# Two-layer mixture-of-experts kernel, first layer's conditioner: load order, sums by parts, slot computation inside the units, three shared blocks behind the pairs

## The chip, the cores and the metric

The kernel runs on one core of one Trainium2 chip. The metric is the device time of one execution in microseconds; the median of three runs stands for the kernel. The profile is of one further execution, whose own time is given beside its span, the time from its first to its last instruction.

## The reference

x holds 32 batches of 128 tokens of width 128. There are two layers, each a conditioner and an FFN, and each adds its result to x. The change touches layer 0's conditioner and its border to layer 0's FFN:

```python
def _L0_cond_ref(context_c, time_cond, ...):
    head, wrist, proprio = context_c[:, :42], context_c[:, 42:84], context_c[:, 84:]
    full_agg = context_c.mean(axis=1)
    hp_agg = concatenate([head, proprio], axis=1).mean(axis=1)
    wp_agg = concatenate([wrist, proprio], axis=1).mean(axis=1)
    gate_logits = concatenate([full_agg, hp_agg, wp_agg], -1) @ gate_w + gate_b
    scale, shift = split(silu(time_cond) @ time_w + time_b, 2, -1)
    gate_scores = softmax(gate_logits * (1.0 + scale) + shift)
    topk_w, topk_i = top_k(gate_scores, 2)          # two of four experts per batch
    topk_w = topk_w / (topk_w.sum(-1) + 1e-08)
    for e in range(4):
        y = gelu(context_c @ ew1[e] + eb1[e]) @ ew2[e] + eb2[e]
        out = out + w_be[:, e] * mask[e] * y        # w_be: topk_w, zero where not chosen
    shared = gelu(context_c @ sw1 + sb1) @ sw2 + sb2
    return out + shared

def _L0_ffn_ref(x, w_router, w_gating, w_gate, w_up, w_down):   # eight experts, all used
    cw = softmax(x @ w_router) * softmax(x @ w_gating / 0.1)
    cw = cw / (sum(cw, -1) + 1e-09)
    return sum over e of cw[:, :, e] * ((silu(x @ w_gate[e]) * (x @ w_up[e])) @ w_down[e])
```

Layer 1 (a second conditioner with routed experts, and a low-rank FFN) is not touched.

## The kernel before

All activations lie transposed, 128 features on the partitions. x is eight blocks of 512 columns, each four batches; `xT[b]` is a block of x, `c0T[b]` the block of the conditioner's output that the FFN reads. All matmuls are in 32-bit floats, so that one matmul of the source is two passes in the trace.

Layer 0's conditioner is a list of units, run by `pipelined`: the up-projection of the next unit is issued before the down-projection of the present one, so that TensorE has matmuls to do while ScalarE works out the GELU. A shared unit (`"s", b`) takes one block through the shared expert: four matmuls (`hidden`, L203, tiles us), each followed by a GELU on ScalarE (L204), then four matmuls summed into one PSUM tile (`project`, L209, tile ys), which VectorE writes to `c0T` (L227). A pair unit (`"p", q`) takes two batches of 128 tokens through one routed expert. Which batches and which expert is only known at run time: 34 pairs of slots are filled from the gates, and the batches' columns are gathered by VectorE (`gather`, L367) and the expert's weights fetched by SyncE's DMA (`fetch`, L357, 578 KB each, three ahead) at addresses held in registers. Results are multiplied by the gate and added to `c0T` (L395).

Slots come from a chain of small steps. `sums` (L197) adds up each batch of x over all tokens, over head with proprio, and over wrist with proprio, as the tokens are sorted head, proprio, wrist. `cond_gates` multiplies these by the gate weights (the gate group on TensorE: gate_ps, mod_ps, t_ps), takes the softmax with an Exp on ScalarE (L257) and chooses two of four (mask, L175). `schedule` counts the choices with two small matmuls (order_ps, L281 and L282), works out each slot's batch, expert and gate on VectorE (up to L321) and spreads them with one matmul (slots_ps, L324) before they are turned to integers (L325 to L328). `spread_times` (tl_ps, L341) prepares a term for layer 1.

The units are shared blocks 0 to 6, the 34 pairs, and shared block 7. The steps of the slot chain are called between units by `after_l0`, after the unit's down-projection: the gates after block 2, the schedule and the first three fetches after block 3, the times after block 4, the first gathers after block 5. Block 7 comes behind the pairs, so its `c0T` begins as zero and its result is added (L225).

The FFN follows: `logits_ahead` (lg_ps, L421) projects blocks 0 to 3 on the gate weights, `ffn_logits` transposes that back (lg_b, L436), `ffn_gates` takes the softmaxes and their product, `gates_to_dram` transposes the result (fg_ps, L450) and stores it, and `fetch_rows` reads it back by rows. Before the change these are called in front of, within and after the first two units of the FFN. 64 FFN units (block, expert) follow, each with eight matmuls up and four down.

Each engine works through its own instructions in order; the order on each engine is set by a scheduler when the kernel is built, near the order of the source. PSUM tiles rotate: six of tag mm (all up-projections and all small matmuls) and two of tag y.

Of the kernel before, what the change touches and what calls it, by code (L numbers as in the profile page):

```python
# [35 lines left out]
ALU = mybir.AluOpType  # L36
AX = mybir.AxisListType
# [54 lines left out]
def adaln_ffn(  # L92
# [19 lines left out]
    def const(shape, name, dtype=F32):  # L112
        return cpool.tile(shape, dtype, tag=name, name=name)
# [14 lines left out]
    c0T = [c0all[:, b * TB : (b + 1) * TB] for b in range(NB)]  # L128
    ident = const([P, P], "ident")

    nc.scalar.dma_start(out=par, in_=packed)
    nc.sync.dma_start(out=xT[0], in_=x[0])
    nc.scalar.dma_start(out=sw1_t, in_=sw1)
    nc.sync.dma_start(out=sw2_t, in_=sw2.rearrange("(c p) d -> p c d", p=P))
    for blk in range(1, NB):
        nc.sync.dma_start(out=xT[blk], in_=x[blk])
    nc.sync.dma_start(out=rows, in_=row.partition_broadcast(P))
    nc.sync.dma_start(out=ident, in_=eye)
# [49 lines left out]
    cT = par[:, AT["cond"]]  # L188
    sT = const([P, B], "sT")
    nc.scalar.activation(sT, cT, AF.Silu)  # L190
    full, hp, wp = (const([P, B], n) for n in ("full", "hp", "wp"))

    def sums(blk):
        xb = batches(xT[blk])
        at = slice(blk * BB, (blk + 1) * BB)
        for to, (lo, hi) in ((full, (0, S)), (hp, NO_WRIST), (wp, NO_HEAD)):
            V.tensor_reduce(to[:, at], xb[:, :, lo:hi], AX.X, ALU.add)  # L197


    def hidden(ps, h, rhs, w, bias):  # L200

        for c in range(NC):
            nc.tensor.matmul(ps[c], lhsT=w[:, c * P : (c + 1) * P], rhs=rhs, start=True, stop=True)  # L203
            nc.scalar.activation(h[:, c, :], ps[c], AF.Gelu_apprx_tanh, bias=bias[:, c : c + 1])  # L204

    def project(w, h, n, name):
        y = y_tile(name)
        for c in range(NC):
            nc.tensor.matmul(y[:, :n], lhsT=w[:, c, :], rhs=h[:, c, :n], start=(c == 0), stop=(c == NC - 1))  # L209
        return y  # L210

    LAST = NB - 1

    def shared_up(blk):
        h = work.tile([P, NC, TB], F32, tag="h", name=f"hs0_{blk}", bufs=3)
        ps = [mm_tile(f"us_{blk}_{c}") for c in range(NC)]
        hidden(ps, h, xT[blk], sw1_t, col("sb1", 0, NC))
        for b in range(3 * blk, min(3 * blk + 3, NB)):
            sums(b)
        return h  # L220

    def shared_down(blk, h):
        y = project(sw2_t, h, TB, f"ys_{blk}")
        if blk == LAST:
            V.scalar_tensor_tensor(c0T[blk], y, col("sb2"), c0T[blk], ALU.add, ALU.add)  # L225
        else:
            V.tensor_scalar(c0T[blk], y, col("sb2"), None, ALU.add)  # L227
# [4 lines left out]
    tsb = const([B, E1], "tsb")  # L232

    def cond_gates():
        V.tensor_scalar(full, full, 1.0 / S, None, ALU.mult)
        V.tensor_scalar(hp, hp, 1.0 / NSEEN, None, ALU.mult)
        V.tensor_scalar(wp, wp, 1.0 / NSEEN, None, ALU.mult)
        gps = mm_tile("gate_ps")
        for i, agg in enumerate((full, hp, wp)):
            nc.tensor.matmul(  # L240
                gps[:B, :E0], lhsT=agg, rhs=col("gate_w", i * E0, E0), start=(i == 0), stop=(i == 2)
            )
        mps = mm_tile("mod_ps")
        nc.tensor.matmul(mps[:B, : 2 * E0], lhsT=sT, rhs=col("time_w", 0, 2 * E0), start=True, stop=True)
        tps = mm_tile("t_ps")
        nc.tensor.matmul(tps[:B, :E1], lhsT=cT, rhs=col("r1t", 0, E1), start=True, stop=True)
        V.tensor_copy(tsb, tps[:B, :E1])
        mod = const([B, 2 * E0], "mod")
        stat = const([B, 4], "stat")
        V.tensor_tensor(gl2, gps[:B, :E0], rows[:B, ATROW["gate_b"]], ALU.add)  # L250
        V.tensor_tensor(mod, mps[:B, : 2 * E0], rows[:B, ATROW["time_b"]], ALU.add)
        V.tensor_scalar(mod[:, :E0], mod[:, :E0], 1.0, None, ALU.add)
        V.tensor_tensor(gl2, gl2, mod[:, :E0], ALU.mult)
        V.tensor_tensor(gl2, gl2, mod[:, E0:], ALU.add)
        V.tensor_reduce(stat[:, 0:1], gl2, AX.X, ALU.max)
        V.tensor_scalar(gl2, gl2, stat[:, 0:1], None, ALU.subtract)
        nc.scalar.activation(gl2, gl2, AF.Exp)  # L257
        V.tensor_reduce(stat[:, 1:2], gl2, AX.X, ALU.add)
        V.reciprocal(stat[:, 2:3], stat[:, 1:2])
        V.tensor_scalar(gl2, gl2, stat[:, 2:3], None, ALU.mult)  # L260
        chosen = top2(gl, B, 1, E0, "c")
        V.tensor_tensor(gl, gl, chosen, ALU.mult)
        V.tensor_reduce(stat[:, 3:4], gl2, AX.X, ALU.add)
        V.tensor_scalar(stat[:, 3:4], stat[:, 3:4], 1e-08, None, ALU.add)
        V.reciprocal(stat[:, 2:3], stat[:, 3:4])
        V.tensor_scalar(gl2, gl2, stat[:, 2:3], None, ALU.mult)

        return chosen.rearrange("p o e -> p (o e)")

# [1 line left out]
    batch_at = const([1, NSLOT], "batch_at", I32)  # L273
    expert_at = const([1, NPAIR + 2], "expert_at", I32)

    def schedule(chosen):


        ps = mm_tile("order_ps")
        earlier = par[:B, AT["earlier"]]  # L280
        nc.tensor.matmul(ps[:B, :E0], lhsT=earlier, rhs=chosen, start=True, stop=True)  # L281
# [19 lines left out]
        shape = [B, E0, NSLOT]  # L301
        at = const(shape, "at")
        part = const(shape, "part")
        sums = const([B, 2 * NSLOT + NPAIR], "sums")
        V.tensor_tensor(
            at, pos.unsqueeze(2).to_broadcast(shape),
            par[:B, AT["slot"]].unsqueeze(1).to_broadcast(shape), ALU.is_equal,
# [11 lines left out]
        V.tensor_scalar(pairs, first[:, 1, :], float(P), None, ALU.mult)  # L319
        for e in range(2, E0):  # L320
            V.scalar_tensor_tensor(pairs, first[:, e, :], float(e * P), pairs, ALU.mult, ALU.add)  # L321
        ps = mm_tile("slots_ps")
        n = sums.shape[-1]
        nc.tensor.matmul(ps[:, :n], lhsT=ones, rhs=sums, start=True, stop=True)  # L324
        V.tensor_copy(batch_at, ps[:1, NSLOT : 2 * NSLOT])  # L325
        V.tensor_copy(expert_at[:, :NPAIR], ps[:1, 2 * NSLOT : n])
        V.tensor_copy(expert_at[:, NPAIR:], ps[:1, n - 2 : n])
        V.tensor_copy(gate_of, ps[:, :NSLOT])  # L328

    tl = const([P, B, E1], "tl")  # L330

# [41 lines left out]
    def pair_up(q):  # L373
        if q + NW - 1 < NPAIR:
            fetch(q + NW - 1)
        if q + AHEAD < NPAIR:
            gather(q + AHEAD)
        w, x = weights[q], slots.pop(q)
        h = work.tile([P, NC, 2 * S], F32, tag="h", name=f"h0_{q}", bufs=3)
        ps = [mm_tile(f"u_{q}_{c}")[:, : 2 * S] for c in range(NC)]  # L380
        hidden(ps, h, x.rearrange("p s t -> p (s t)"), w[:, ATP["w1"]], w[:, ATP["eb1"]])
        return h

    def pair_down(q, h):
# [7 lines left out]
        for i, at in enumerate(batch.pop(q)):  # L392
            acc = c0all[:, bass.ds(at, S)]
            s = 2 * q + i
            V.scalar_tensor_tensor(acc, t[:, i, :], gate_of[:, s : s + 1], acc, ALU.mult, ALU.add)  # L395

    def after_l0(kind, i):
        if (kind, i) == ("s", 2):
            held["chosen"] = cond_gates()
        if (kind, i) == ("s", 3):  # L400
            schedule(held["chosen"])
            for q in range(NW - 1):
                fetch(q)
        if (kind, i) == ("s", 4):
            spread_times()
        if (kind, i) == ("s", 5):
            for q in range(AHEAD):
                gather(q)

    held, in_dram = {}, {}  # L410
    L0 = {"s": (shared_up, shared_down), "p": (pair_up, pair_down)}
    units = [("s", b) for b in range(LAST)] + [("p", q) for q in range(NPAIR)] + [("s", LAST)]
    nc.gpsimd.memset(c0T[LAST], 0.0)
    pipelined(units, lambda k, i: L0[k][0](i), lambda k, i, h: L0[k][1](i, h), after_l0)

    lg = const([P, NT, 2 * EF], "lg")

# [69 lines left out]
        )  # L487
        held["f", sb] = cwT


    def fetch_rows(blk):

        sb, j = divmod(blk, SB)
        t = work.tile([P, 2, TB], F32, tag="gT", name=f"fgT{blk}")
        for k in range(4):
            nc.sync.dma_start(
                out=t[32 * k : 32 * k + 1, :, :], in_=in_dram["f", sb][k : k + 1, :, j * TB : (j + 1) * TB]
            )
        return t

    def spread(row, name):

# [6 lines left out]
        nc.scalar.activation(s, ps_gate, AF.Silu)  # L509
        V.tensor_tensor(h, s, ps_up, ALU.mult)  # L510

    fgates = {}
    l1 = const([P, NT, E1], "l1")

    def ffn_up(blk, e):
        h = work.tile([P, NC, TB], F32, tag="h", name=f"hf_{blk}_{e}", bufs=3)
        for c in range(NC):
            if (blk, e, c) == (0, 0, 1):
                ffn_logits(0)
            cs = slice(c * P, (c + 1) * P)  # L520
            g, u = mm_tile(f"g_{blk}_{e}_{c}"), mm_tile(f"u_{blk}_{e}_{c}")
            nc.tensor.matmul(g, lhsT=wg_t[:, e, cs], rhs=c0T[blk], start=True, stop=True)  # L522
            nc.tensor.matmul(u, lhsT=wu_t[:, e, cs], rhs=c0T[blk], start=True, stop=True)  # L523
            glu(g, u, h[:, c, :], f"sf_{blk}_{e}_{c}")
        if (blk, e) == (0, 0):
            ffn_gates(0)
        if (blk, e) == (0, 1):
            gates_to_dram("f", 0)
            fgates[0] = fetch_rows(0)
        return h  # L530

    def ffn_down(blk, e, h):
# [72 lines left out]
        V.tensor_scalar(flat[:, : 4 * 32], ps[:, : 4 * 32], 0.125, None, ALU.mult)  # L605
        V.tensor_scalar(flat[:, 4 * 32 :], ps[:, 4 * 32 : 12 * 32], 0.25, None, ALU.mult)

    logits_ahead("lg", par[:, AT["wr"]], c0T, 0)
    pipelined([(b, e) for b in range(NB) for e in range(EF)], ffn_up, ffn_down, after_ffn)


# [200 lines left out]
```

## Time and profile before

| | |
|---|---|
| median of three runs | 1021.22 us (1020.12 to 1021.42) |
| profiled execution, its own time | 1021.55 us |
| its span | 1019.6 us |
| TensorE busy | 1004.8 us, 99% |
| VectorE busy | 460.4 us, 45% |
| ScalarE busy | 332.6 us, 33% |
| GpSimd busy | 145.7 us, 14% |
| mean granted TensorE clock | 0.997 |
| read from HBM | 31.76 MB |

In the profile's rows PE is TensorE, PEld its weight loads, DVE VectorE, ACT ScalarE, POOL GpSimd and SP SyncE; a q behind the name is the engine's sequencer, which issues DMAs. L209 is line 209 of the kernel. A row of the timeline is a start, a length, the engine, the line, the operation, its output and inputs with their shapes, how many instructions it stands for, and in brackets how long the engine had been idle and what ended that. The stages of the span are: the conditioner of layer 0 up to about 186 us (shared blocks to 58 us, pairs to 183 us), the FFN up to 853 us, layer 1 from there.

### The profile page before, as it was taken

To read this page: it belongs to the slowest core of one execution; us is meant where nothing else is said; L and a number is where in the kernel's file an instruction comes from. 1 tells how busy PE (TensorE), PEld (TensorE's weight loads), DVE (VectorE), ACT (ScalarE), POOL (GpSimd) and SP (SyncE) were. 2 spreads that over 40 slices of the span, in tenths; PEclk is the share of its full clock that TensorE was granted. 3 is DMA by queue.
4 is the path that set the end of the run, shared out by engine and by line. 5 is a ranking of instruction groups with operands and counts; after the bars stand their busy time and mean duration, and the time that the engine had idled before them with its cause. 6 is when DMAs were issued, how large, how long until landed. Compare 5 with 4: busy or idle time off the path is not lost.

```text
span 1019.6 us, 10200 instructions
## 1 busy us (share of the span) xinstructions
PE 1004.8 (99%) x3662; PEld 478.4 (47%) x3662; DVE 460.4 (45%) x811; ACT 332.6 (33%) x575; POOL 145.7 (14%) x142
## 2 busy tenths in 40 slices
PE   7999999999999999999999999999999999999997
PEld 3368888444445444444444444444444443333341
DVE  5434443445443444333445534344433344638692
ACT  4444544423221222222223222222222222335764
POOL 0000000031111111111111101111111002008770
PEclk9999999999999999999999999999999999999999
DMA  9335555100000000000000000000000000000002
GB/s 315 106 103 179 165 176 167 34 2 1 3 2 0 1 0 1 1 1 1 0 1 1 1 3 1 0 1 0 1 0 1 0 1 3 2 6 1 2 1 82
DMA packets 18705, 34.76 MB, mean 34 GB/s; under 512 B 1680, under 2 KB 9872, under 8 KB 18640
## 3 DMA queue, kind: packets, MB, share of 16 engines
q1 hardware_dynamic: 17792, 32.61, 9.9%
q10 hardware_dynamic: 864, 1.52, 0.4%
q8 instruction: 28, 0.46, 0.2%
q14 instruction: 21, 0.17, 0.1%
HBM read 31.76 MB, written 2.36 MB: 33 GB/s over the span
## 4 chain that ended last, share of the span: by engine, by line
PE 98%; DVE 1%; DMA 0%; DVEq 0%; issue 0%; ACTq 0%
PE yf L209 22%; PE g L522 22%; PE u L523 22%; PE u L203 6%; PE y L209 6%; PE ur L625 5%; PE us L203 3%; PE g L625 3%; PE u L625 3%; PE ys L209 2%; PE p_ps L619 2%; PE ul L676 1%; PE q_ps L619 1%; DMA sw_t<-in_sw 0%; PE fold_ps L603 0%; PE o_ps L691 0%
## 5 line engine op out<-in xcount | busy, mean ns | idle before, releaser
L509 ACT ACTIVATE sf<-g 128x512 f32<-128x512 f32 x256 | 152.6, 597 | 495.5 <-PE g L522 494.3
L510 DVE TENSOR_TENSOR hf<-sf,u 128x512 f32<-128x512 f32 x256 | 175.7, 687 | 207.2 <-PE u L523 206.2
L522 PE MATMUL g<-c0all,wg_t 128*128 128x512 f32 x512 | 261.6, 592 | 0.0
L523 PE MATMUL u<-c0all,wu_t 128*128 128x512 f32 x512 | 261.4, 592 | 0.0
L209 PE MATMUL yf<-hf,wd_t 128*128 128x512 f32 x512 | 230.5, 593 | 0.0
L504 POOL PARTITION_BROADCAST fg<-fgT x64 | 77.8, 1227 | 721.1 <-DVE tf L536 516.6
L209 PEld LDWEIGHTS yf<-hf,wd_t 128*128 128x128 f32 x512 | 97.1, 190 | 123.0 <-issue 123.0
L523 PEld LDWEIGHTS u<-c0all,wu_t 128*128 128x128 f32 x512 | 97.3, 190 | 122.4 <-issue 120.3
L522 PEld LDWEIGHTS g<-c0all,wg_t 128*128 128x128 f32 x512 | 96.7, 190 | 120.5 <-issue 118.3
L536 DVE TENSOR_TENSOR tf<-yf,fg 128x512 f32<-128x512 f32 x64 | 44.2, 691 | 167.5 <-PE yf L209 162.0
L504 POOL PARTITION_BROADCAST rg<-grows x64 | 66.7, 1168 | 123.3 <-DVE hr L659 73.5
L204 ACT ACTIVATE h<-u,w 128x256 f32<-128x256 f32 x136 | 58.5, 473 | 62.2 <-PE u L203 62.2
L659 DVE TENSOR_TENSOR hr<-ar,rg 128x512 f32<-128x512 f32 x64 | 59.9, 981 | 15.9 <-ACT ar L658 15.4
L203 PE MATMUL u<-x,w 128*128 128x256 f32 x272 | 64.3, 379 | 0.0
L209 PE MATMUL y<-h,w 128*128 128x256 f32 x272 | 64.3, 379 | 0.0
L625 PE MATMUL ur<-xall,rw_t 128*32 128x512 f32 x512 | 58.4, 592 | 0.0
L203 PEld LDWEIGHTS u<-x,w 128*128 128x128 f32 x272 | 51.7, 190 | 7.9 <-issue 1.0
L209 PEld LDWEIGHTS y<-h,w 128*128 128x128 f32 x272 | 51.7, 190 | 7.4 <-issue 0.5
L658 ACT ACTIVATE ar<-ur 128x512 f32<-128x512 f32 x64 | 37.9, 598 | 27.6 <-PE ur L625 27.3
L537 DVE TENSOR_TENSOR xall<-xall,tf 128x512 f32<-128x512 f32 x64 | 45.4, 709 | 2.1
L625 PE MATMUL g<-xall,sws_t 128*32 128x512 f32 x256 | 42.0, 593 | 0.0
L625 PE MATMUL u<-xall,sws_t 128*32 128x512 f32 x256 | 42.0, 592 | 0.0
(168 smaller groups left out, 449.6 us busy)
## 6 DMA issues: line engine op xcount, KB each, us to landing
w<-in_experts SPq DMA_DIRECT2D x34, 578.5 KB
xall<-in_x SPq DMA_DIRECT2D x8, 256.0 KB
wg_t<-in_w_gate SPq DMA_DIRECT2D x8, 256.0 KB
wu_t<-in_w_up SPq DMA_DIRECT2D x8, 256.0 KB
wd_t<-in_w_down SPq DMA_DIRECT2D x8, 256.0 KB
rw_t<-in_r_w SPq DMA_DIRECT2D x2, 512.0 KB
out<-fin SPq DMA_DIRECT2D x4, 256.0 KB
out<-fin ACTq DMA_DIRECT2D x4, 256.0 KB
```

The lines of the kernel that those rows point to most:

```text
L203: nc.tensor.matmul(ps[c], lhsT=w[:, c * P : (c + 1) * P], rhs=rhs, start=True, stop=True)
L204: nc.scalar.activation(h[:, c, :], ps[c], AF.Gelu_apprx_tanh, bias=bias[:, c : c + 1])
L209: nc.tensor.matmul(y[:, :n], lhsT=w[:, c, :], rhs=h[:, c, :n], start=(c == 0), stop=(c == NC - 1))
L504: nc.gpsimd.partition_broadcast(bc, row)
L509: nc.scalar.activation(s, ps_gate, AF.Silu)
L510: V.tensor_tensor(h, s, ps_up, ALU.mult)
L522: nc.tensor.matmul(g, lhsT=wg_t[:, e, cs], rhs=c0T[blk], start=True, stop=True)
L523: nc.tensor.matmul(u, lhsT=wu_t[:, e, cs], rhs=c0T[blk], start=True, stop=True)
L536: V.tensor_tensor(t, y, spread(fgates[blk][32 * k : 32 * k + 1, g, :], f"fg_{blk}_{e}"), ALU.mult)
L537: V.tensor_tensor(xT[blk], xT[blk], t, ALU.add)
L625: nc.tensor.matmul(ps[own, :], lhsT=w[:, own], rhs=x, start=True, stop=True)
L659: V.tensor_tensor(h[:, j, :], a, gate, ALU.mult)
```

## The change

It has four parts.

1. First loads: on ScalarE's queue sw1 is issued before par (the packed small inputs); on SyncE's queue x's second block is issued before sw2.
2. Sums: each block is summed over head, proprio and wrist apart, in all of blocks 0 to 3 with shared unit 0 and 4 to 7 with shared unit 1; three additions form the three sums that the gates need.
3. Steps between: a table `between` names points inside a unit, ahead of a given chunk of a given up- or down-projection, and the steps are called there. The gates are called in the middle of block 2's up-projection, the schedule ahead of block 3's up-projection, the slots' spreading (now `spread_slots`, with the fetches and the gathers) ahead of the last chunk of block 2's down-projection, the times inside block 3's down-projection.
4. Order of units: blocks 0 to 4, the pairs, then blocks 5, 6 and 7. Three blocks begin as zeros and are added to. The FFN's first gates are worked out within these three units instead of in the first FFN units.

```diff
+    nc.scalar.dma_start(out=sw1_t, in_=sw1)
+    nc.sync.dma_start(out=xT[0], in_=x[0])
     nc.scalar.dma_start(out=par, in_=packed)
-    nc.sync.dma_start(out=xT[0], in_=x[0])
-    nc.scalar.dma_start(out=sw1_t, in_=sw1)
+    nc.sync.dma_start(out=xT[1], in_=x[1])
     nc.sync.dma_start(out=sw2_t, in_=sw2.rearrange("(c p) d -> p c d", p=P))
-    for blk in range(1, NB):
+    for blk in range(2, NB):
...
-        for to, (lo, hi) in ((full, (0, S)), (hp, NO_WRIST), (wp, NO_HEAD)):
-            V.tensor_reduce(to[:, at], xb[:, :, lo:hi], AX.X, ALU.add)
+        lo = 0
+        for to, n in ((head, NHEAD), (prop, NPROP), (wrist, NHEAD)):
+            V.tensor_reduce(to[:, at], xb[:, :, lo : lo + n], AX.X, ALU.add)
+            lo += n
...
+    between = {}
+
+    def before(*point):
+        for do in between.pop(point, ()):
+            do()
...
         for c in range(NC):
+            before("up", *unit, c)
             nc.tensor.matmul(ps[c], lhsT=w[:, c * P : (c + 1) * P], rhs=rhs, start=True, stop=True)
...
         for c in range(NC):
+            before("down", *unit, c)
             nc.tensor.matmul(y[:, :n], lhsT=w[:, c, :], rhs=h[:, c, :n], start=(c == 0), stop=(c == NC - 1))
...
-        for b in range(3 * blk, min(3 * blk + 3, NB)):
-            sums(b)
+        if blk < 2:
+            for b in range(4 * blk, 4 * blk + 4):
+                sums(b)
...
     def cond_gates():
+        V.tensor_tensor(hp, head, prop, ALU.add)
+        V.tensor_tensor(wp, wrist, prop, ALU.add)
+        V.tensor_tensor(full, hp, wrist, ALU.add)
...
+    def spread_slots():
         ps = mm_tile("slots_ps")
...
         V.tensor_copy(gate_of, ps[:, :NSLOT])
+        for q in range(NW - 1):
+            fetch(q)
+        for q in range(AHEAD):
+            gather(q)
...
-    def after_l0(kind, i):
-        if (kind, i) == ("s", 2):
-            held["chosen"] = cond_gates()
-        if (kind, i) == ("s", 3):
-            schedule(held["chosen"])
-            for q in range(NW - 1):
-                fetch(q)
-        if (kind, i) == ("s", 4):
-            spread_times()
-        if (kind, i) == ("s", 5):
-            for q in range(AHEAD):
-                gather(q)
-    units = [("s", b) for b in range(LAST)] + [("p", q) for q in range(NPAIR)] + [("s", LAST)]
-    nc.gpsimd.memset(c0T[LAST], 0.0)
...
+    def first_rows():
+        gates_to_dram("f", 0)
+        fgates[0] = fetch_rows(0)
+
+    between.update({
+        ("up", "s", 2, 2): [cond_gates],
+        ("up", "s", 3, 0): [schedule],
+        ("down", "s", 2, 3): [spread_slots],
+        ("down", "s", 3, 1): [spread_times],
+
+        ("up", "s", FIRST + 1, 2): [lambda: logits_ahead("lg", par[:, AT["wr"]], c0T, 0)],
+        ("down", "s", FIRST, 0): [lambda: ffn_logits(0)],
+        ("down", "s", FIRST, 3): [lambda: ffn_gates(0)],
+        ("down", "s", FIRST + 1, 0): [first_rows],
+    })
+    units = [("s", b) for b in range(FIRST)] + [("p", q) for q in range(NPAIR)]
+    units += [("s", b) for b in range(FIRST, NB)]
+    for b in range(FIRST, NB):
+        nc.gpsimd.memset(c0T[b], 0.0)
...
-            if (blk, e, c) == (0, 0, 1):
-                ffn_logits(0)
...
-        if (blk, e) == (0, 0):
-            ffn_gates(0)
-        if (blk, e) == (0, 1):
-            gates_to_dram("f", 0)
-            fgates[0] = fetch_rows(0)
...
-    logits_ahead("lg", par[:, AT["wr"]], c0T, 0)
```

`FIRST` is `NB - 3`, block 5.

More of the change, by code (lines that the diff above doesn't have):

```diff
@@ L190, in adaln_ffn @@
     nc.scalar.activation(sT, cT, AF.Silu)
-    full, hp, wp = (const([P, B], n) for n in ("full", "hp", "wp"))
+    full, hp, wp, head, prop, wrist = (const([P, B], n) for n in ("full", "hp", "wp", "hd", "pr", "wr"))
     def sums(blk):
@@ L195, in sums, with hidden, project @@
         at = slice(blk * BB, (blk + 1) * BB)
-        for to, (lo, hi) in ((full, (0, S)), (hp, NO_WRIST), (wp, NO_HEAD)):
-            V.tensor_reduce(to[:, at], xb[:, :, lo:hi], AX.X, ALU.add)
-    def hidden(ps, h, rhs, w, bias):
+        lo = 0
[6 more added lines that the diff above has]
+            do()
+    def hidden(ps, h, rhs, w, bias, unit):
         for c in range(NC):
+            before("up", *unit, c)
             nc.tensor.matmul(ps[c], lhsT=w[:, c * P : (c + 1) * P], rhs=rhs, start=True, stop=True)
             nc.scalar.activation(h[:, c, :], ps[c], AF.Gelu_apprx_tanh, bias=bias[:, c : c + 1])
-    def project(w, h, n, name):
+    def project(w, h, n, name, unit=()):
         y = y_tile(name)
         for c in range(NC):
+            before("down", *unit, c)
             nc.tensor.matmul(y[:, :n], lhsT=w[:, c, :], rhs=h[:, c, :n], start=(c == 0), stop=(c == NC - 1))
         return y
-    LAST = NB - 1
+    FIRST = NB - 3
     def shared_up(blk):
@@ L216, in shared_up @@
         ps = [mm_tile(f"us_{blk}_{c}") for c in range(NC)]
-        hidden(ps, h, xT[blk], sw1_t, col("sb1", 0, NC))
-        for b in range(3 * blk, min(3 * blk + 3, NB)):
-            sums(b)
+        hidden(ps, h, xT[blk], sw1_t, col("sb1", 0, NC), ("s", blk))
+        if blk < 2:
+            for b in range(4 * blk, 4 * blk + 4):
+                sums(b)
         return h
     def shared_down(blk, h):
-        y = project(sw2_t, h, TB, f"ys_{blk}")
-        if blk == LAST:
+        y = project(sw2_t, h, TB, f"ys_{blk}", ("s", blk))
+        if blk >= FIRST:
             V.scalar_tensor_tensor(c0T[blk], y, col("sb2"), c0T[blk], ALU.add, ALU.add)
@@ L266, in cond_gates @@
         V.tensor_scalar(gl2, gl2, stat[:, 2:3], None, ALU.mult)
-        return chosen.rearrange("p o e -> p (o e)")
+        held["chosen"] = chosen.rearrange("p o e -> p (o e)")
     gate_of = const([P, NSLOT], "gate_of")
@@ L274, in adaln_ffn, with schedule @@
     expert_at = const([1, NPAIR + 2], "expert_at", I32)
-    def schedule(chosen):
+    slot_sums = const([B, 2 * NSLOT + NPAIR], "slot_sums")
+    def schedule():
+        chosen = held["chosen"]
         ps = mm_tile("order_ps")
@@ L303, in schedule @@
         part = const(shape, "part")
-        sums = const([B, 2 * NSLOT + NPAIR], "sums")
+        sums = slot_sums
         V.tensor_tensor(
@@ L321, in schedule @@
             V.scalar_tensor_tensor(pairs, first[:, e, :], float(e * P), pairs, ALU.mult, ALU.add)
+    def spread_slots():
         ps = mm_tile("slots_ps")
-        n = sums.shape[-1]
-        nc.tensor.matmul(ps[:, :n], lhsT=ones, rhs=sums, start=True, stop=True)
+        n = slot_sums.shape[-1]
+        nc.tensor.matmul(ps[:, :n], lhsT=ones, rhs=slot_sums, start=True, stop=True)
         V.tensor_copy(batch_at, ps[:1, NSLOT : 2 * NSLOT])
@@ L380, in pair_up @@
         ps = [mm_tile(f"u_{q}_{c}")[:, : 2 * S] for c in range(NC)]
-        hidden(ps, h, x.rearrange("p s t -> p (s t)"), w[:, ATP["w1"]], w[:, ATP["eb1"]])
+        hidden(ps, h, x.rearrange("p s t -> p (s t)"), w[:, ATP["w1"]], w[:, ATP["eb1"]], ("p", q))
         return h
@@ L395, in pair_down @@
             V.scalar_tensor_tensor(acc, t[:, i, :], gate_of[:, s : s + 1], acc, ALU.mult, ALU.add)
-    def after_l0(kind, i):
-        if (kind, i) == ("s", 2):
-            held["chosen"] = cond_gates()
-        if (kind, i) == ("s", 3):
-            schedule(held["chosen"])
-            for q in range(NW - 1):
-                fetch(q)
-        if (kind, i) == ("s", 4):
-            spread_times()
-        if (kind, i) == ("s", 5):
-            for q in range(AHEAD):
-                gather(q)
-    held, in_dram = {}, {}
-    L0 = {"s": (shared_up, shared_down), "p": (pair_up, pair_down)}
-    units = [("s", b) for b in range(LAST)] + [("p", q) for q in range(NPAIR)] + [("s", LAST)]
-    nc.gpsimd.memset(c0T[LAST], 0.0)
-    pipelined(units, lambda k, i: L0[k][0](i), lambda k, i, h: L0[k][1](i, h), after_l0)
     lg = const([P, NT, 2 * EF], "lg")
@@ L499, in fetch_rows @@
         return t
+    held, in_dram, fgates = {}, {}, {}
+    def first_rows():
[11 more added lines that the diff above has]
+    })
+    L0 = {"s": (shared_up, shared_down), "p": (pair_up, pair_down)}
+    units = [("s", b) for b in range(FIRST)] + [("p", q) for q in range(NPAIR)]
+    units += [("s", b) for b in range(FIRST, NB)]
+    for b in range(FIRST, NB):
+        nc.gpsimd.memset(c0T[b], 0.0)
+    pipelined(units, lambda k, i: L0[k][0](i), lambda k, i, h: L0[k][1](i, h))
     def spread(row, name):
@@ L510, in glu @@
         V.tensor_tensor(h, s, ps_up, ALU.mult)
-    fgates = {}
     l1 = const([P, NT, E1], "l1")
```

## The prediction

> **What bounds the kernel now.** I read the busy shares first, then TensorE's waits, then the chain of work that ended last through the first 60 us, then the windows around its one long wait.
>
> The page's head says that TensorE is the bound: it is busy for all but 14.8 us of the span.
>
> ```profile
> span 1019.6 us, 10200 instructions
> ...
> PE 1004.8 (99%) x3662; PEld 478.4 (47%) x3662; DVE 460.4 (45%) x811; ACT 332.6 (33%) x575; POOL 145.7 (14%) x142
> ```
>
> So only TensorE's idle time, and its slow time, can be won. Its waits (who waited for what: us in total, times, longest) are three:
>
> ```profile
> PE us L203 <- DMA sw_t<-in_sw: 5.7, 1, 5.7
> PE slots_ps L324 <- DVE sums L321: 2.0, 1, 2.0
> PE o_ps L691 <- DVE qT L687: 0.8, 1, 0.8
> ```
>
> The third is at the very end and not touched. The chain (start, length, what) shows the other two:
>
> ```profile
> 1.17 4.40 DMA sw_t<-in_sw
> 5.57 0.14 issue
> 5.71 8.76 PE us L203 x16
> ...
> 35.67 3.45 PE ys L209 x8
> ...
> 44.91 0.55 PE slots_ps L324 x2
> 45.46 5.33 PE us L203 x8
> 50.79 0.62 PE tl_ps L341 x2
> 51.41 3.63 PE us L203 x8
> ```
>
> The reader is to see two things. The first matmul starts at 5.71 when sw1 is in. And the same eight passes of an up-projection take 5.33 us after the slots wait and 3.63 us one unit later. The windows explain it (length, busy time by engine, granted clock, DMA share, GB/s):
>
> ```profile
> 42.94:44.91 1.97, 0.01 (x1) 0.00 (x0) 1.88 (x7) 0.00 (x0) 0.00 (x0) 1.00 0.00 0
> 43.16:46.58 3.42, 1.67 (x5) 0.97 (x6) 2.23 (x11) 0.00 (x0) 0.00 (x0) 1.00 0.00 0
> 46.58:49.99 3.41, 3.41 (x5) 1.33 (x4) 1.08 (x7) 1.58 (x3) 0.00 (x0) 0.50 0.66 232
> 50.00:53.41 3.41, 3.41 (x9) 1.35 (x8) 1.19 (x6) 1.89 (x4) 0.00 (x0) 1.00 0.97 361
> ```
>
> TensorE is idle for 1.97 us while VectorE works out the slots; for the following 3.41 us the granted clock is 0.50. So the wait costs 1.97 us and then 5.33 - 3.63 = 1.70 us more.
>
> **The change, part by part.**
>
> *First loads (-1.05 us).* On ScalarE's queue sw1 now stands ahead of par. In the chain, sw1 is issued at 1.17 behind par's 205 KB and in use 4.40 us later, at 5.57. Par alone was issued at 0.73 and used at 4.25 (row below), 3.52 us. The 256 KB behind it ended 1.32 us later, 5.2 ns per KB; so sw1, 51 KB more than par, would be in at 0.73 + 3.52 + 0.27 = 4.52 and the first matmul starts at 4.66, after the same 0.14 of issue. x's first block was in use at 4.05 with the same place on its queue, so it isn't the later one.
>
> ```profile
> 4.05 0.69 DVE L197 TENSOR_REDUCE full<-xall 128x4 f32<-128x512 f32 x1 [4.05 <-DMA xall<-in_x]
> 4.25 0.23 ACT L190 ACTIVATE sT<-par 128x32 f32<-128x32 f32 x1 [1.31 <-DMA par<-in_packed]
> ```
>
> Par is then late: about 0.73 + 4.84 = 5.57. ScalarE waits for it with SiLU (0.23) and a table load (1.28) before its first GELU, so about 7.1; the first tile is finished 2.08 us after the first matmul (5.71 to 7.79 before), at 6.74. Those 0.4 us cost nothing: six PSUM tiles let TensorE run on until its seventh, six tiles later, and the GELU at 0.69 keeps pace with a tile at 0.86. sw2, moved behind x's second block, is wanted only by the first down-projection at about 13.4.
> The early matmuls run at half rate (the first tile took 2.08 us, later ones 0.86). [...] Bounds: -0.5 to -1.35 (x's block as the only limit, 4.05 + 0.14 + 0.17). I take -1.05.
>
> *Sums by parts (0).* Before, 24 reductions over 512, 344 and 344 elements start 0.60, 0.42 and 0.42 us apart; slope 0.18/168 us per element puts 168 or 176 elements at about 0.24, so a block takes 0.72 instead of 1.44. Now all eight blocks come in the first two units. The last block's data were issued at 5.6 us and VectorE never waited for them after 6.37; in the new order they end near 10.4, so the sums end near 11, with three additions and three scalings (the old scalings, L235 to L237, start 0.09 us apart) near 12. The gate matmuls want them at 18.6. Even old reductions would end in time; the cover is 6 us.
>
> *Slots in mid-unit (-1.97 and -1.70).* The new order on TensorE, from the built kernel: two units up, ys_0, two chunks of us_2, the gate group, two chunks, ys_1, order_ps, us_3, three chunks of ys_2, slots_ps. Let X be the start of the gate group (4.66 + 8.76 + 3.43 + 1.72 = 18.57). TensorE reaches order_ps at X + 0.41 (the group) + 1.72 + 3.43 = X + 5.56. Is the mask there? The old rows:
>
> ```profile
> 33.61 0.22 DVE L256 TENSOR_SCALAR gl<-gl,stat 32x4 f32<-32x4 f32 x1
> 34.70 1.28 ACT L257 ACT_TABLE_LOAD   x1
> 35.99 0.20 ACT L257 ACTIVATE gl<-gl 32x4 f32<-32x4 f32 x1
> 37.78 0.16 DVE L175 TENSOR_SCALAR maskc<-rankc 32x4 f32<-32x4 f32 x1
> ```
>
> The old X is 31.56, the mask ends at X + 6.38. The Exp stood behind two GELUs of the next unit (until 34.68, X + 3.12) and its table load. Now it stands behind one (from X + 1.57 to X + 2.26), so load, Exp and all behind them come 0.86 earlier: mask at X + 5.52. TensorE arrives at X + 5.56: no wait, with 0.04 us to spare. What queues behind: VectorE does four more small operations (0.72), evicts ys_1 (0.67), then L283 (0.2), then from the copy of n to the last of L321 4.45 us without the eviction that stood inside (39.81 to 44.86 is 5.05, less 0.67; 0.07 for the pair): X + 5.52 + 0.72 + 0.67 + 0.2 + 4.45 = X + 11.56. TensorE arrives at slots_ps at X + 5.56 + 0.22 + 3.43 + 2.57 = X + 11.78: 0.22 us to spare. So the wait of 1.97 is gone, but by margins of tenths; an error of half a microsecond in either shows as a wait of that size. I add +0.1, bounds 0 to +1.0.
> Clock: the row says 1.97 us idle, 51% of a 3.41 us window, was followed by a window at 0.50. [...] Three runs spread over 1.30 us (1020.12 to 1021.42) and the profiled one is the highest: I weigh 1.70 by 0.85, -1.45.
>
> *What follows the slots (0).* slots_ps comes at 18.57 + 11.8 = 30.4. SyncE's first fetch of a pair's weights was issued 1.68 us after slots_ps began (44.91 to 46.59), so at 32.1. It is moved ahead by 14.5 us, past nothing that isn't issued: the old loads of FFN weights have drained by then.
>
> ```profile
> 30.00:32.00 2.00, 2.00 (x15) 0.80 (x13) 0.33 (x1) 0.00 (x0) 0.00 (x0) 1.00 0.28 66
> 32.00:34.00 2.00, 2.00 (x7) 1.02 (x6) 1.69 (x10) 0.70 (x2) 0.00 (x0) 1.00 0.00 0
> ```
>
> Four fetches (2.37 MB) took from 46.59 to about 54.3 before, so the first is in near 36. The first pair's matmul comes after a chunk of ys_2, us_4, ys_3, tl_ps (0.62) and a chunk of ys_4, 9.5 us after slots_ps: 39.9. Cover 3.9 us. The gathers (0.16 each) end within 3 us.
>
> *Three blocks behind the pairs (0).* The FFN gates were hidden before: TensorE has no wait between 45 and 1012 us. Moved, lg_ps follows y_33 by two chunks (1.72); the last pair's eviction and two additions end 1.3 us after y_33 (182.80 to 184.06): 0.4 to spare. lg_b again has two chunks of cover. From lg_b to the finished gates took 8.6 us (189.6 to 198.2) with six FFN multiplications (3.9) among them and an Exp waiting on SiLUs; without these, with ys_5's eviction, about 5.4; fg_ps comes 6.9 after lg_b. Hidden; if not, a wait of under 1 us. Two more memsets (0.51) on an idle GpSimd.
>
> **Sum.** -1.05 - 1.97 - 1.45 + 0.1 = -4.37 from the median, 1021.22: 1016.85. From the profiled execution (1021.55, its span 1019.6 and 1.95 around it), with the full 1.70: 1016.93. I say 1016.9.
>
> **The rivals.**
> Only the wait goes, not the clock loss, because most timed runs never paid it, or the start gains nothing: 1018.3 or 1018.0. [...] against: the row.
> A wait in its place: order_ps or slots_ps late by 1 us and more, as the margins are 0.04 and 0.22; above some 1.7 us in one window it takes the 1.70 of clock along. 1.7 + 1.7: 1020.3, no measurable change.
> Slower: the first pair's weights come late. The price is their landing after 39.9, one for one, plus 1.70 of clock; from about 3.7 us late (43.6, 11.5 us after issue) it is slower than no change by the 2 us that can be told; 6 us late gives 1024.6. Against: the same fetch, on an empty queue, took under 4 us.
> That the change doesn't do what it says: the built order has each group where the text puts it.
>
> **How the numbers follow.** Likeliest 0.74 (1015.5 to 1017.9 by its own bounds), clock or start not won 0.14, a new wait 0.08, late weights 0.04. About 0.2%, 2 us, is what can be told from no change. Faster: the first two, 0.88; same 0.08; slower 0.04. The range reaches down for a start at its best bound and up to the second case with 0.4 of new wait: 1015.2 to 1018.7.
>
> **What would show it.** First matmul at 4.4 to 4.9; no slots_ps line over 0.5 us in TensorE's waits; no window at 0.50 between the start and the last 5 us; the first pair's matmul near 40. Wrong: a wait on maskc, slots or w, or a first matmul after 5.3.

## The result and the profile after

The changed kernel takes 1016.98 us (median of seven runs, 1016.14 to 1017.88) against 1021.31 us before (1020.12 to 1021.68, seven runs): ratio 0.996, 95% interval 0.9949 to 0.9972. Predicted were 1016.9 us, and 1015.2 to 1018.7 as the range. The profiled execution took 1017.31 us, its span 1015.5.

TensorE's waits after the change (who waited for what: us in total, times, longest):

```profile
PE us L215 <- DMA sw_t<-in_sw: 4.5, 1, 4.5
PE o_ps L713 <- DVE qT L709: 0.8, 1, 0.8
```

The wait of 2.0 us for the slots is gone, and nothing stands in its place; the first wait is 1.2 us shorter. The chain of work that ended last, through the stage that was changed (start, length, what):

```profile
0.73 3.77 DMA sw_t<-in_sw
4.49 0.04 issue
4.54 9.67 PE us L215 x16
14.20 3.43 PE ys L222 x8
17.64 1.72 PE us L215 x4
19.35 0.28 PE gate_ps L257 x6
...
25.11 0.15 PE order_ps L301 x2
25.26 0.06 PE order_ps L302 x2
25.33 3.63 PE us L215 x8
28.96 2.57 PE ys L222 x6
31.53 0.48 PE slots_ps L346 x2
32.01 1.05 PE ys L222 x2
33.07 3.43 PE us L215 x8
```

From 4.54 us on TensorE has no gap, and the eight passes of the up-projection that follows slots_ps (33.07) take 3.43 us; in the kernel before the eight behind it took 5.33. But the first sixteen passes take 9.67 us, and 8.76 before: the early start is nearly lost again in this pair of profiles (the up-projections end at 14.20, before at 14.46). The trace's clock records say why: the first rise of the clock is at 9.67 us here and was at 9.03, so TensorE worked 5.13 us at half rate in this execution and 3.32 in that. (The windows view gives 1.00 for the time before the first record; that the rate is half there is read from the passes themselves. Shortest, median and longest, in ns, over the first 20 us of the kernel before:)

```profile
L203 PE MATMUL us<-xall,sw_t x22: 592/592/1192, 5.7 to 19.9; 128*128 128x512 f32 x22
```

How long the start is slow differs between executions of one kernel (3.32, 4.40 and 3.98 us in the three profiles of the kernel before, in the table below), which is why a comparison of the two spans (4.1 us) must not be read part by part.

The two margins, VectorE's results against TensorE's arrival:

```profile
19.28 0.23 PE L257 MATMUL gate_ps<-par,full 128*32 128x4 f32 x2
...
24.65 0.16 DVE L176 TENSOR_SCALAR maskc<-rankc 32x4 f32<-32x4 f32 x1
25.04 0.22 PE L301 MATMUL order_ps<-maskc,par 32*32 32x4 f32 x2
...
30.37 0.40 DVE L341 SCALAR_TENSOR_TENSOR slot_sums<-at,slot_sums 32x34 f32<-32x34 f32 x2
31.46 0.55 PE L346 MATMUL slots_ps<-slot_sums,ones 32*128 32x170 f32 x2
```

The gate group's first pass is at X = 19.28. The mask ends at 24.81, X + 5.53, and TensorE's order_ps follows at 25.04; the slots are ready at 30.77 and slots_ps starts at 31.46. So both come in time, by 0.23 and 0.69 us. (The chain above dates the same passes 0.07 us later, from the end of the record before them.)

### The profile page after: what moved, and what is told of

It is laid out like the page before. It is cut to its first block, busy times and chain, and to the rows that moved or that the text cites. A ratio compares the mean times of both kernels' runs of the same rounds, so it can differ in the third digit from the quotient of the medians.

```text
span 1015.5 us, 10214 instructions
## 1 busy us (share of the span) xinstructions
PE 1003.9 (99%) x3662; PEld 478.1 (47%) x3662; DVE 455.8 (45%) x814; ACT 332.8 (33%) x575; POOL 146.8 (14%) x144
## 4 chain that ended last, share of the span: by engine, by line
PE 99%; DMA 0%; DVE 0%; DVEq 0%; issue 0%
PE yf L222 22%; PE g L550 22%; PE u L551 22%; PE y L222 6%; PE u L215 6%; PE ur L647 5%; PE us L215 3%; PE g L647 3%; PE ys L222 3%; PE u L647 3%; PE p_ps L641 2%; PE ul L698 1%; PE q_ps L641 1%; DMA sw_t<-in_sw 0%; PE fold_ps L626 0%; PE o_ps L713 0%
```

## The experiments

**Each part by itself.** First the new load order alone, in the kernel before:

```diff
-    nc.scalar.dma_start(out=par, in_=packed)
-    nc.sync.dma_start(out=xT[0], in_=x[0])
     nc.scalar.dma_start(out=sw1_t, in_=sw1)
+    nc.sync.dma_start(out=xT[0], in_=x[0])
+    nc.scalar.dma_start(out=par, in_=packed)
+    nc.sync.dma_start(out=xT[1], in_=x[1])
     nc.sync.dma_start(out=sw2_t, in_=sw2.rearrange("(c p) d -> p c d", p=P))
-    for blk in range(1, NB):
+    for blk in range(2, NB):
```

> The kernel before with the new load order alone. Theory: the first matmul comes at about 4.6 instead of 5.7 us and, [...] the whole 1.05 us shows on average: 1021.3 - 1.05 = 1020.3 us. Rival, the cold clock lasts until a fixed moment and half of the start is spent at half rate: 1020.8. Rival, the start is worth nothing: 1021.3. The wait for slots_ps stays at 2.0 us in each.

Measured: 1019.71 us beside 1021.05 before, ratio 0.9986 (0.9979 to 0.9992). Its chain begins:

```profile
0.73 3.63 DMA sw_t<-in_sw
4.36 0.04 issue
4.40 8.68 PE us L204 x16
```

The first matmul came 1.3 us earlier than before's 5.71, and 1.34 us were won (0.8 to 2.1 by the interval): the whole of it, as the theory said, not half, which would be 0.65.

Then the changed kernel with the old load order (the same diff the other way):

> The changed kernel with the old load order: the slots in mid-unit without the earlier start. Theory: 1017.0 + 1.05 = 1018.0 us, no wait for slots_ps and no window at half clock between the start and the end. Rival (half of the start is spent at half rate): 1017.5. If the wait and its clock loss were worth only the 1.97 us of the wait: 1019.3.

Measured: 1017.99 us beside 1021.05, ratio 0.997 (0.9959 to 0.9981), no wait for slots_ps and no slow window between the start and the end. So the slots in mid-unit are worth 3.06 us. The interval, 1.9 to 4.2 us, is too wide to tell that from the 3.4 that I gave to wait and clock together, or from the wait alone; the table below parts them. The old load order costs the changed kernel 1.01 us (1017.99 against 1016.98), as predicted.

The fourth part undone: one block behind the pairs, the FFN gates where they were.

```diff
-    FIRST = NB - 3
+    FIRST = NB - 1
...
-        ("up", "s", FIRST + 1, 2): [lambda: logits_ahead("lg", par[:, AT["wr"]], c0T, 0)],
-        ("down", "s", FIRST, 0): [lambda: ffn_logits(0)],
-        ("down", "s", FIRST, 3): [lambda: ffn_gates(0)],
-        ("down", "s", FIRST + 1, 0): [first_rows],
...
+            if (blk, e, c) == (0, 0, 1):
+                ffn_logits(0)
...
+        if (blk, e) == (0, 0):
+            ffn_gates(0)
+        if (blk, e) == (0, 1):
+            first_rows()
...
+    logits_ahead("lg", par[:, AT["wr"]], c0T, 0)
```

> The changed kernel with its fourth part undone: one shared block behind the pairs, and layer 0's FFN gates back in the first FFN units. Theory: moving these was worth nothing, 1017.0 us, within 0.3. Rival, the three blocks hide something that I did not see: 0.6 us or more above the changed kernel, with a wait of TensorE near the border of pairs and FFN.

Measured: 1016.66 us (five runs, 1016.27 to 1017.19), and only the two waits of TensorE that the changed kernel has. Its executions lie among those of the changed kernel; the part is worth nothing that can be told.

The sums as they were, 24 long reductions:

```diff
-        lo = 0
-        for to, n in ((head, NHEAD), (prop, NPROP), (wrist, NHEAD)):
-            V.tensor_reduce(to[:, at], xb[:, :, lo : lo + n], AX.X, ALU.add)
-            lo += n
+        for to, (lo, hi) in ((full, (0, S)), (hp, NO_WRIST), (wp, NO_HEAD)):
+            V.tensor_reduce(to[:, at], xb[:, :, lo:hi], AX.X, ALU.add)
...
-        V.tensor_tensor(hp, head, prop, ALU.add)
-        V.tensor_tensor(wp, wrist, prop, ALU.add)
-        V.tensor_tensor(full, hp, wrist, ALU.add)
```

> The changed kernel with the old reductions over 512, 344 and 344 elements, all in the first two units. Theory: they end near 16.5 us, the gate matmuls want them at 19.3, so nothing waits: 1017.0 us within 0.3. Rival, the sums by parts are what lets the gates come in time: a wait of TensorE in front of gate_ps.

Measured: 1016.65 us (five runs, 1016.35 to 1017.52). The last reduction, and what stands behind it up to the gate group:

```profile
15.30 0.50 DVE L198 TENSOR_REDUCE wp<-xall 128x4 f32<-128x344 f32 x1
17.71 0.75 DVE L239 TENSOR_SCALAR c0all<-ys,par 128x512 f32<-128x512 f32 x1 [1.91 <-PE ys L220]
...
18.55 0.17 DVE L249 TENSOR_SCALAR wp<-wp 128x32 f32<-128x32 f32 x1
19.32 0.23 PE L252 MATMUL gate_ps<-par,full 128*32 128x4 f32 x2
```

The sums end at 15.8 us, 3.5 before the gate group. But their scalings stand behind the eviction of ys_0 on VectorE, so what the gate group reads is ready at 18.72, only 0.6 us ahead of it; in the changed kernel it is ready at 12.4. So the sums by parts bring nothing to the time, but they widen this margin by over 6 us.

**Is the slow clock a consequence of the wait?** The kernel before with the gap filled by work that nobody reads:

```diff
+        idle = mm_tile("idle_ps")
+        for _ in range(2):
+            nc.tensor.matmul(idle, lhsT=sw1_t[:, :P], rhs=xT[0], start=True, stop=True)
         ps = mm_tile("slots_ps")
```

> The kernel before with two matmuls of 0.86 us, whose result nobody reads, ahead of the wait for slots_ps. The slots come no earlier, so the wait itself is still paid, but TensorE is idle for about 0.3 us instead of 1.97. Theory (the half clock after the wait is a consequence of the idle time): 1.45 us less than before on average, 1019.9 us, and the eight passes behind slots_ps take 3.6 us instead of 5.3. Rival, [...] the slow window had another cause: 1021.3, as before.

Measured: 1020.03 us beside 1021.05, ratio 0.999 (0.9983 to 0.9996): 1.02 us less, not 1.45. Its chain:

```profile
40.24 1.91 PE idle_ps L324 x4
42.15 3.43 PE ys L209 x8
45.59 0.48 PE slots_ps L327 x2
46.07 3.63 PE us L203 x8
```

The passes behind slots_ps are at full rate after nearly the same wasted time. Not all of the 1.02 us is clock: slots_ps starts 5.57 us after order_ps (39.95 to 45.52) and 5.88 before (39.03 to 44.91), 0.31 us sooner, since the eviction of ys_4 (0.67 us in the midst of VectorE's chain before) now comes after it. That leaves about 0.7 us, within the interval of 0.4 to 1.7 for the whole.

The other way round, the changed kernel with a wait put back:

```diff
+        same = const([B, 2 * NSLOT + NPAIR], "same")
+        V.tensor_scalar(same, slot_sums, 0.0, 1.0, ALU.mult, ALU.add)
+        for _ in range(5):
+            V.reciprocal(same, same)
+        V.tensor_tensor(slot_sums, slot_sums, same, ALU.mult)
+
     def spread_slots():
```

> The changed kernel with five reciprocals of ones put into the slot chain on VectorE, which leave the sums as they are but end about 7 us later; in the built order TensorE does ys_2 and ys_3 first and then stands idle for about 2.9 us in front of slots_ps. Theory: the wait is paid one for one and clock with it, in the executions in which at least half of one window of 3.41 us falls into the idle time (about 85% of phases, 1.45 us on average): 1017.0 + 2.9 + 1.45 = 1021.3 us. Rival[...]: 1019.9, and no window at half clock after the wait.

Measured: 1020.91 us beside 1021.01 before, ratio 1.0 (0.9992 to 1.0008): 3.9 us over the changed kernel, for a wait of 2.7 us. But its profile had no slow window after the wait. Twice more, for the profile:

> The changed kernel with the delayed slot chain, once more for its profile. Its first profile showed the wait of 2.7 us and no half clock after it, with a window's border falling near the middle of the idle time. Theory: with another phase of the windows, more than half of one window falls into the idle time and the next 3.41 us run at half clock; by its medians this is so in about two of three executions. Rival [...]: no such window.

> The same once more. Theory: a window at half clock after the wait if, counted from the first rise of the clock in steps of 3.413 us, one step has over half of its length in the idle time; none if the idle time is cut near its middle. Rival: none in any case.

Both, at 1021.45 and 1021.25 us, had one. The windows of these three, cut from the first rise of the clock in steps of 3.413 us, the length of the record at half clock in the first profile of the kernel before (length, busy time by engine, granted clock, DMA share, GB/s). The first profile:

```profile
34.32:37.73 3.41, 1.91 (x5) 0.57 (x3) 3.38 (x5) 0.00 (x0) 0.00 (x0) 1.00 0.00 0
37.73:41.15 3.42, 2.17 (x6) 1.16 (x7) 2.23 (x10) 0.47 (x1) 0.00 (x0) 1.00 0.00 0
41.15:44.56 3.41, 3.41 (x9) 1.35 (x8) 1.23 (x7) 2.28 (x4) 0.00 (x0) 1.00 0.82 303
```

The second:

```profile
36.04:39.46 3.42, 1.36 (x4) 0.78 (x5) 2.49 (x7) 0.00 (x0) 0.00 (x0) 1.00 0.00 0
39.46:42.87 3.41, 3.41 (x5) 1.35 (x4) 1.13 (x7) 1.37 (x2) 0.00 (x0) 0.50 0.59 205
42.87:46.28 3.41, 3.41 (x9) 1.35 (x8) 1.19 (x6) 1.37 (x2) 0.00 (x0) 1.00 0.97 360
```

The third:

```profile
35.58:38.99 3.41, 1.10 (x4) 0.68 (x5) 2.73 (x8) 0.00 (x0) 0.00 (x0) 1.00 0.00 0
38.99:42.40 3.41, 3.41 (x6) 1.35 (x5) 1.14 (x8) 1.38 (x2) 0.00 (x0) 0.50 0.54 168
```

In the first, TensorE's busy time in the two steps that share the idle time is 1.91 and 2.17 of 3.41: no loss. In the others one step holds most of it and has 1.36 and 1.10: the next step is at half clock.

The kernel before, twice more, to see whether the half clock follows its wait each time:

> The kernel before once more, for its profile. Theory: the 1.97 us wait for slots_ps is there again at the same length; [...] it may be absent, with the time then in the lower half of 1020.1 to 1021.8 us unless the start was slow for longer. Rival (the half clock is an effect of that place in the program): always there, 3.4 us long.

> The kernel before, a third profile. Theory: time less half of the slow time at the start, less 1.71 us if half clock follows the wait, is 1018.2 us, as in the two others (1021.55 - 1.66 - 1.71 = 1018.2 and 1020.5 - 2.2 = 1018.3). Rival (something else differs between executions): another rest.

Measured: 1020.5 and 1020.15 us, each with the wait of 2.0 us and without a slow window after it. Of the first (the idle time, then the step that holds most of it, then the next):

```profile
43.43:45.41 1.98, 0.00 (x1) 0.00 (x1) 1.89 (x7) 0.00 (x0) 0.00 (x0) 1.00 0.00 0
44.20:47.61 3.41, 2.20 (x6) 1.16 (x7) 2.22 (x13) 0.50 (x1) 0.00 (x0) 1.00 0.00 0
47.61:51.02 3.41, 3.41 (x9) 1.35 (x8) 1.23 (x7) 2.25 (x4) 0.00 (x0) 1.00 0.84 286
```

So the same wait in the same kernel costs the clock in one execution and not in another. The fetches' DMA, which begins in the same stretch, is no rival cause: its share is 0.66 in the slow window of the kernel before (46.58 to 49.99) and 0.84 here, at full clock. With this, executions can be compared. "Slow at start" is from the first matmul that the kernel needs to the first rise in the trace's clock records; half of it is lost, and half of a slow window of 3.41. What remains of the own time:

| kernel | own time | slow at start | idle time in front of slots_ps, as the step's border cuts it | slow window after | rest |
|---|---|---|---|---|---|
| before | 1021.55 | 3.32 | 0.21 + 1.75 | yes | 1018.18 |
| before, second | 1020.50 | 4.40 | 0.76 + 1.22 | no | 1018.30 |
| before, third | 1020.15 | 3.98 | 0.55 + 1.42 | no | 1018.16 |
| new loads alone | 1020.30 | 3.15 | 0.11 + 1.86 | yes | 1017.02 |
| old loads | 1017.99 | 3.99 | none | no | 1016.00 |
| changed | 1017.31 | 5.13 | none | no | 1014.74 |
| one block behind | 1017.19 | 4.68 | none | no | 1014.85 |
| old sums | 1017.36 | 5.34 | none | no | 1014.69 |
| gap filled | 1020.56 | 5.15 | none | no | 1017.98 |
| late slots | 1020.67 | 5.82 | 1.50 + 1.24 | no | 1017.76 |
| late slots, second | 1021.45 | 4.20 | 0.68 + 2.06 | yes | 1017.64 |
| late slots, third | 1021.25 | 3.69 | 0.43 + 2.31 | yes | 1017.70 |

The rest of a kernel that was profiled three times agrees within 0.15 us, while its own times lie up to 1.4 apart; what differs between executions is the clock, as far as this can tell.

**How often the clock was lost.** The timed executions have their mean granted clock on record too, to three decimals; it counts the start as full speed, so it shows the slow window after the wait and the slow stretch at the very end (0.50 over the last 3.6 us in the first profile of before). In the profiles of before it is 0.9965 with the window and 0.9975 and 0.9976 without. Of 61 further executions of the kernel before, 6 have 0.996 and so the window, 39 have 0.998 and so not. The 16 at 0.997 fall into two groups by their time: eleven take 1021.49 to 1021.83 us and five 1020.09 to 1020.36, with none between. With the window, the rest of 1018.2 and its 1.71 us make 1019.9, which leaves the five a slow start of under 1 us; without it, the eleven would need one of over 6.5. The profiles have 3.15 to 5.82. So the eleven had the window and the five had not: 17 of 61 in all, which is an estimate, of 0.5 us on average. Read the same way, the window came in 6 of 21 executions of the new loads alone, in 7 of 13 of the late slots (0.9 us on average, which with the 3.0 us between the rests makes the 3.9 measured), and in none of the 21 with the gap filled.

The table also suggests why it came so seldom. A start that is slow for longer delays the wait by only half of that. From the first profile of before to the second it was slow for 1.08 us longer (3.32 to 4.40), and the step's border moved into the wait by 0.55 (0.21 to 0.76). By an estimate from these two rows, a start that is slow for more than some 4 us leaves the border inside the wait, which it splits into two parts that are each shorter than the 1.75 us behind which the clock was lost. The table agrees. Among the profiles of before and of the new loads, the slow window follows a slow start of 3.15 and 3.32 us, and not one of 3.98 and 4.40; among those of the late slots, whose wait is longer, it follows 3.69 and 4.20, and not 5.82.

**A version that beats both.** The same accounts put the cost of the half clock at the start at some 2 us (half of the table's 3.15 to 5.82, counted from the first matmul). If work that nobody reads brings the rise of the clock forward, part of that can be won while the first loads are on their way. So four matmuls on a tile of ones, with a result that is not read, go in front of the changed kernel:

```diff
+    blank = const([P, 256], "blank")
+    V.memset(blank, 1.0)
+    idle = mm_tile("idle_ps")
+    for _ in range(4):
+        nc.tensor.matmul(idle[:, :256], lhsT=blank[:, :P], rhs=blank, start=True, stop=True)
```

> The changed kernel with four matmuls on a tile of ones at the very start, before the first loads are in; they take about 3.4 us at half rate, their result is not read. Theory: [...] it ends some 3.4 us earlier; half of that is won: 1017.0 - 1.7 + 0.1 (the last of them may hold up the first real matmul) = 1015.4 us. Rival, the clock comes up at a time that has nothing to do with TensorE's work: 1017.0 or 0.1 above.

Measured: 1015.59 us (1014.84 to 1016.04) beside 1021.01 before, ratio 0.9946 (0.9932 to 0.9959). That is 1.4 us under the changed kernel by the medians, 1.1 when each is taken against its own executions of before; the intervals of the two ratios overlap, but all five executions (1014.84 to 1016.04) lie below all seven of the changed kernel. Its chain, and the row of the timeline for the first needed passes:

```profile
1.18 3.78 PE idle_ps L193 x8
4.96 7.71 PE us L221 x16
12.67 3.43 PE ys L228 x8
...
4.75 7.91 PE L221 MATMUL us<-xall,sw_t 128*128 128x512 f32 x16
```

The sixteen passes take 7.71 us instead of 9.67 in the chain, since the clock rose at 6.44 us, 1.7 us after the first of them, 5.26 us after the first of the idle work and 3.2 us earlier than in the profile of the changed kernel (9.67); that first needed pass begins at 4.75, 0.2 us later than in the changed kernel, behind the last of the idle work. The rest is 1015.82 - 0.85 = 1014.97, the changed kernel's 1014.74 and those 0.2 us.

## Why the prediction was right

The time was right to 0.1 us; its terms were not all so. Against the rests in the table:

- *First loads, -1.05.* The rest falls by 1.2 us with the new order, from 1018.2 to 1017.0; the first matmul came at 4.54 and 4.40, not 4.66. That all of it would show in the median although it is spent at half rate, and not half of it (the bound of -0.5), was my estimate; the medians bear it out. A pair of profiles shows another amount, as happened here (slow at start for 3.32 us before, 5.13 after). The step from par's 3.52 us plus 0.27 for 51 KB more erred by 0.1 to 0.3 on the safe side. The two comparisons of medians give 1.34 and 1.01 us. This also rules out the rival that the start gains nothing.
- *The wait, -1.97.* The rest falls by 2.2 us (1018.2 to 1016.0 with the old loads). Of the 0.2 that I missed, 0.16 is overlap: matmul records lap over the next by that much in a stream (592 ns each, and eight passes take 3.43 us), so that a gap of 1.97 between two records stands for 2.13 from start to start. The rest is not traced.
- *The clock, -1.45.* This is the step that was mis-sized. That the half clock comes with the idle time is shown by the filled gap, by the late slots and by the three profiles of before; the size is not 0.85 of 1.70. By the count above the window came in 17 of 61 executions, not in 85%, and cost 0.5 us on average. The medians less the rests say the same more coarsely: they are 2.85 us for before (1021.05 - 1018.2) and 1.8 to 2.2 us for the kernels without a wait, 0.6 to 1.1 us apart. I had read the spread of three runs as the slow window coming and going, but the changed kernel, which has no such wait, spreads as widely (1.74 us), from the start alone. I took the profiled execution for the usual one. And I took the place of a step's border in the wait for chance, when it goes with the length of the slow start (0.21 us into the wait after 3.32, 0.55 after 3.98, 0.76 after 4.40). (The 51% of a window in the forecast is the 1.75 us that fell into one step; the whole 1.97 is 58%.)
- *New waits, +0.1.* None. The mask came at X + 5.53, predicted X + 5.52, and the slots at X + 11.49, predicted X + 11.56. TensorE came later than I had it, by 0.2 and 0.4, since the passes of an up-projection behind a group of small matmuls take 0.2 us longer (1.91 against 1.72, 3.63 against 3.43). The forecast showed such a row of 3.63 and reckoned with 3.43. With its own arrival times the margins would have been 0.03 and 0.29 us, so part of the room is luck.
- *Sums, moved FFN gates, moved fetches, 0.* Shown for the first two by undoing them; the last by the wait list alone. The first fetch was issued at 33.13 us and the first pair's matmul came at 41.61 (forecast 39.9), with no wait. (In the rival of late weights a sum is off: 3.7 us late and 1.7 of clock make 1022.3, only 1.1 us slower than no change; 2 us slower takes 4.6.) The FFN gates came in time by less than forecast:

```profile
173.57 0.75 DVE L239 SCALAR_TENSOR_TENSOR c0all<-ys,par,c0all 128x512 f32<-128x512 f32 x1 [0.94 <-PE ys L222]
174.24 0.34 DVE L486 RECIPROCAL sm<-sm 128x32 f32<-128x32 f32 x1
...
176.22 0.38 DVE L492 TENSOR_TENSOR cwT<-cw,sm 128x128 f32<-128x128 f32 x1
176.81 0.27 PE L457 MATMUL fg_ps<-ident,cwT 128*128 128x128 f32 x1
```

The forecast had the gates done 5.4 us after lg_b (169.50) and fg_ps at 6.9. They took 7.1, because the softmax's reciprocal (L486) stood on VectorE behind an eviction that was itself waiting for TensorE; fg_ps came at 7.3, with 0.2 us to spare in place of 1.5.

Summed with the measured sizes: -1.2 - 2.2 - 0.5 = -3.9 by the count, and -4.5 at most by the medians. The forecast was -4.37. Measured were -4.33 against the seven executions of before in the result, and -4.07 against the median of the 61 others (1021.05). An over-sized clock term, two under-sized ones and the draw of the executions made up for each other; the forecast was right in its mechanism, and lucky in coming within 0.1 us. On the clock the rival of 1018.3, that most executions never paid the loss, was nearer to the truth than its chance of 0.14 said: 44 of 61 did not pay it.

## What to carry to other kernels

In a kernel that TensorE bounds, look for its few waits and let the work of other engines that ends them begin a unit earlier, by calling it inside a unit rather than after it; then check the margins operation by operation. On VectorE's slot chain that held here to a few hundredths of a microsecond; where an eviction that must wait stood ahead of a chain, it was 1.7 us off. Here a wait of TensorE of 1.97 us cost 1.7 us of clock beside itself, but only in some executions (17 of 61, by the estimate above): count them by the granted clock of every timed execution, and do not trust the one profile. And the idle time before the first data was of use here: work that nobody reads, put into it, took 1.4 us off the median.

## What the runs showed of the hardware

- *Half clock after a wait of TensorE.* In steps of 3.413 us from the first rise of the clock, the steps with 1.75 us (before), 1.86 (new loads alone), 2.06 and 2.31 (late slots, second and third profile) of idle time were followed by a step at 0.50. Those with at most 1.22 us (before, second), 1.42 (before, third) and 1.50 (late slots, first) were followed by one at 1.00. With no wait in that place (gap filled) the eight passes behind it took 3.63 us, where they took 5.33 before.
- *Where the clock changed.* By the clock records, in the first profile of before the clock fell 37.55 us after its first rise and rose again 3.41 us later; in the second of the late slots it fell 30.72 us after the first rise, and in the changed kernel only at the end, 1003.52 us after it. These are 11, 1, 9 and 294 times 3.413 us.
- *The start.* The first rise came 3.15 to 5.82 us after the first needed matmul in the table's twelve profiles, 4.4 us on average; half of that, 2.2 us, is an estimate of what the start costs.
- *Work whose result nobody reads.* With four matmuls on a constant tile from 1.18 us on, the clock rose 1.7 us after the first needed matmul; in the twelve profiles without them it never rose less than 3.15 us after it.
